# The last block's tail of a Perceiver kernel: state space prepared two pieces at a time, the perceptron begun ahead of it, its later matrices made behind its first products

## The chip, the cores and the metric

The kernel runs on one core of one Trainium2 chip. TensorE (PE), VectorE (DVE), ScalarE (ACT), GpSimd (POOL) and SyncE (SP, which issues most of the DMAs) each work through their own queue in order, and wait for each other by semaphores. The metric is the time of one execution on the device in microseconds; a kernel's time is the median of several runs. All times inside an execution are microseconds from the start of its span.

## What is computed

The network has four layers on x, 16 sequences of 64 tokens with 256 features (1024 tokens in all). Each layer is a cross attention over a context, a sequence mixer and a feed-forward part, each added to x behind a layer norm. Only the last layer matters here. Cut to that:

```python
x = x + L3_xattn(_layernorm(x), ctx)          # 8 heads of 64, 1024 keys
x = x + L3_attn(_layernorm(x))                # a state space (Mamba) block
x = x + L3_ffn(_layernorm(x))                 # a perceptron with +1/-1 matrices

# L3_attn: 512 inner channels, 16 states each
u, x_gate = split(x @ in_proj_w)              # 256 -> 512 + 512
u = silu(conv3(u) + conv_b)                   # along the 64 tokens of a sequence
delta, b, c = split(u @ x_proj_w)             # 512 + 16 + 16
delta = softplus(delta @ dt_proj_w + dt_proj_b)
h_t = exp(delta_t * a) * h_{t-1} + delta_t * b_t * u_t    # a scan over tokens
y_t = sum over the 16 states of h_t * c_t
y = (y + u * D_param) * silu(x_gate) @ out_proj_w         # 512 -> 256

# L3_ffn: kernels are booleans, w = where(kernel, 1, -1)
h = s0 * (concat([x, -x]) @ w0)               # -> 1024
h = s1 * ((relu(h) * 2) @ w1)                 # 1024 -> 1024
h = s2 * ((relu(h) * 2) @ w2)                 # 1024 -> 256
```

## The kernel before

x stays on chip as `xs`, eight tiles of 128 tokens by 256 features. The state space and the perceptron work on chunks of 256 tokens (two tiles), four chunks in all. The function `L3` runs the last layer in two phases.

In the first phase `heads64` does the attention tile by tile, and calls `go` four times a step, so that the state space of chunks already attended to runs in the gaps. In the second phase, the tail, the attention is done. `dense_setup` makes the perceptron's matrices, and then the perceptron of chunk 0, 1, 2 and 3 follows. A loop calls `go` until the state space is done with the chunk that the perceptron needs, and then once at each `yield` of the perceptron, so that what is left of chunk 2 and the whole of chunk 3 run between the perceptron's products:

```python
ssm.rate = 1.5
dense = self.dense_setup()
for i in range(0, NT, 2):
    while ssm.done < i + 2:
        ssm.go()
    for _ in dense(i, 2):
        ssm.go()
```

`go` does two things. It advances the preparation of the next chunk (`prepare`) by one piece, up to the next `yield`. And it adds `rate` to a credit, and for each whole unit of credit advances the running chunk by one item (`items`). The preparation is: norm (L1919), transposes and copies to `hTs` (L1923), eight products with the input matrix, with the convolution on VectorE (L1934, L1939) and copies on ScalarE, a Silu over all of it (L1946), the product for b and c, written to memory as `bcs` (L1953), four delta products (L1961, L1962), then the softplus: Exp (L1964), Ln (L1965), an addition on VectorE (L1966), four multiplications on GpSimd (L1969), each followed by a DMA that writes delta and delta times u to memory as `dus` (L1970).

A chunk has 32 items: eight slots of four. A slot reads its rows of `dus` back, each repeated over partitions (`rep<-dus`, L1980, eight DMAs a slot, fetched one slot ahead into four `rep` tiles); b and c come back repeated as `bc_rep` (L1992). An item is two decays on ScalarE (`da`, L2010), a product (L2016), a scan (L2020) and a product (L2023) on VectorE. Its result lies in one of six tiles `x`, taken in turn. The four results of a slot are summed on TensorE by 8 small products with `stack` (`add_up`, L2044), issued behind the second item of the next slot; so the third and fourth item of that slot take the tiles that this sum's first half sets free. After every second slot VectorE combines the sum with u and the gate (`v`, L2050, and L2051). After the last, the output product (L69 `halves<-ug`/`w,ug`) is added to x (`add_to_x`, L89), and the chunk is done.

The perceptron of a chunk (`dense`) is: norm and transposes to `hT`, layer one with 8 column blocks of 2 products, layer two with 8 blocks of 8, layer three with 2 blocks of 8, all 128 x 128 by 256 columns in float32; the profile shows two rows for each product. A block of layers one and two lands in one of four PSUM tiles `ps_h` and is taken by a relu, on ScalarE for even blocks (L2105) and on VectorE for odd ones (L2103). Layer three is added to x by VectorE (L2133), and each tile goes out by a DMA (L2136).

The perceptron's matrices come as bytes. `pack_L3_ffn` loads them into a tile of the weight ring when `dense_setup` asks for them. Then VectorE makes w0 (L2089, two pieces), ScalarE w1 (L2093, eight pieces of 128 x 1024), VectorE w2 (L2094).

The order on TensorE is the order in which the program issues, as is the work by hand in `L3` (`manual_schedule`); on the other engines and on SP's queue a scheduler may move instructions past each other.

Of the kernel before, what the change touches and what calls it, by code (L numbers as in the profile page):

```python
# [13 lines left out]
U8 = mybir.dt.uint8  # L14
# [18 lines left out]
RING = 7296  # L33
# [9 lines left out]
class Net:  # L43
# [376 lines left out]
    def heads64(  # L420
# [5 lines left out]
        nc = self.nc  # L426
        wq, wkT, wvT, wo, bo, wvo, wvo2 = self.pack()
        large = large or self.misc
        self.n_pT = 3
# [1391 lines left out]
    def pack_L3_attn(self):  # L1821

        self.slot()
        shape = {n: self.a[f"L3a_{n}"].shape for n in ("in", "bc", "out")}
        return self.carve(*shape["in"]), self.carve(128, 4, 512), self.carve(*shape["bc"]), self.carve(*shape["out"])

    def pack_L3_ffn(self):
        t = self.ring.tile([128, 4 * RING], U8, tag="w", name="w")
        got, at = [], 0
        for name, c, f in (("L3f_k0", 4, 1024), ("L3f_k1", 8, 1024), ("L3f_k2", 8, D)):  # L1830
            v = t[:, at : at + c * f].rearrange("p (c f) -> p c f", f=f)
            at += c * f
            self.nc.sync.dma_start(v, self.a[name])
            got.append(v)
        return got

    def L3(self, ctx_pool):
        tc, nc = self.tc, self.nc
        with ExitStack() as stack:
# [10 lines left out]
            with (  # L1850
                tc.tile_pool(name="sb_L3x", bufs=1, side="left", reuse_waits="tile") as self.lp,
                tc.tile_pool(name="ps_L3x", bufs=1, space=PSUM, reuse_waits="tile") as self.lps,
            ):
                self.heads64(
                    lambda shape: self.lps.tile(shape, F32, tag="t", bufs=2, name="large"),
                    ssm.go, ssm.more, ssm.first,
                )
            ctx_pool.__exit__(None, None, None)
            self.lp = pool("sb_L3f", bufs=1, side="left")
            self.lps = pool("ps_L3f", bufs=1, space=PSUM)  # L1860
            ssm.rate = 1.5
            dense = self.dense_setup()
            for i in range(0, NT, 2):
                while ssm.done < i + 2:
                    ssm.go()
                for _ in dense(i, 2):
                    ssm.go()

    def state_space(self):
        nc = self.nc  # L1870
        N = 16
        w = []
        s = SimpleNamespace(ready=0, done=0, rate=1.1, credit=0.0, prepared=0, started=0)
        al = self.sb.tile([128, 4 * N], F32, name="al")
# [31 lines left out]
        def weights():  # L1906
            for n, to in zip(("in", "bc", "out"), (w[0], w[2], w[3])):
                nc.sync.dma_start(to, self.a[f"L3a_{n}"])
            yield

        def prepare(k):
            win, wdt, wbc, _ = w
            ug = ugs[k % 2]
            os = []
            for t in range(2):
# [3 lines left out]
                nc.vector.tensor_scalar(os[t], x, mv[:, 0:1], rs, ALU.subtract, ALU.mult)  # L1919
            yield  # L1920
            hT = self.sb.tile([128, 2, CHUNK], F32, tag="hTs", name="hTs")
            for t in range(2):
                nc.scalar.copy(hT[:, :, t * 128 : (t + 1) * 128], self.transposed(os[t]))  # L1923
            yield
            up = self.act.tile([128, 4, 4, S + 2], F32, tag="hT", name="up")
# [20 lines left out]
            nc.scalar.activation(ug, ug, AF.Silu)  # L1946
            yield
            yield
            ps = self.misc([32, CHUNK])
# [131 lines left out]
    def dense_setup(self):  # L2081
        nc = self.nc
        k0, k1, k2 = self.pack()

# [6 lines left out]
        nc.vector.memset(minus, -1.0)  # L2091
        for c in range(8):
            nc.scalar.activation(w1[:, c, :], k1[:, c, :], AF.Identity, bias=minus, scale=2.0)  # L2093
        nc.vector.tensor_scalar(w2, k2, 2.0, -1.0, ALU.mult, ALU.add)  # L2094

# [11 lines left out]
        def dense(first, tiles):  # L2107
            hT = self.lp.tile([128, 2, CHUNK], F32, tag="hT", bufs=1, name="hT")
            for t in range(tiles):
# [4 lines left out]
                self.evict(hT[:, :, t * 128 : (t + 1) * 128], self.transposed(o))  # L2114
            yield

            def layer(name, w, x, chunks, k):
                r = self.lp.tile([128, 8, CHUNK], F32, tag=name, bufs=1, name=name)
                for m in range(8):
# [3 lines left out]
                    if m % 2 or chunks > 2:  # L2123
                        yield
                return r
# [3 lines left out]
            for t in range(tiles):  # L2129
# [6 lines left out]
                nc.sync.dma_start(out[:, i, :], self.xs[:, i, :])  # L2136
                yield

# [61 lines left out]
    def run(self, layers):  # L2200
# [8 lines left out]
            "L2_ffn": (self.L2_ffn, [self.pack_L2_gate] + [lambda e=e: self.pack_L2_expert(e) for e in range(E)]),  # L2209
            "L3": (None, [lambda: self.pack_heads64("L3"), self.pack_L3_attn, self.pack_L3_ffn]),  # L2210
        }
# [188 lines left out]
```

## Time and profile before

| | |
|---|---|
| median of three runs | 2966.4 us (2960.71 to 2970.5) |
| the profiled execution, whole | 2962.24 us |
| its span, first to last instruction | 2960.5 us |
| TensorE busy over the span | 2687.8 us, 91% |
| VectorE, ScalarE, GpSimd busy | 1462.2, 1045.9, 302.6 us |
| mean granted TensorE clock | 0.949 |
| last attention product ends at | 2698.24 us |
| last perceptron product ends at | 2957.20 us |

A line of a timeline gives start, length, engine, source line, operation, the written tile and the read ones, and how often; in square brackets stands how long the engine was idle before it and who released it. The windows give the busy time of each engine in a stretch of the span and the clock that TensorE was granted there, as a share of full speed. The chain that ended last is the work that, followed back from the last instruction, ended each wait.

### The profile page before, as it was taken

The page shows a single profiled execution, that of the slowest core. Times are in us where ns is not written, and L with a number is a line of the kernel's source. Part 1 is how long each engine was busy: PE and PEld are TensorE (multiplying, and loading weights), DVE is VectorE, ACT ScalarE, POOL GpSimd, SP SyncE. Part 2 cuts the span into 40 slices and gives each one's busy share as a digit, 9 for nine tenths or more (in the row PEclk, how much of TensorE's full clock was granted, in tenths as well). Part 3 has the DMA queues.
Part 4 walks back from the last instruction along what each step waited for, and adds up shares of the span by engine and source line. Part 5 has one row for each costly group of instructions (what it writes and reads, how often), then busy time and mean ns, then how long its engine had stood idle before and what let it go on. Part 6 is the DMA issues. An engine that isn't in the chain of part 4 may idle for free. (4 is left out here: it accounts for less than half of the span.)

```text
span 2960.5 us, 42845 instructions
## 1 busy us (share of the span) xinstructions
PE 2687.8 (91%) x16972; PEld 1979.6 (67%) x16972; DVE 1462.2 (49%) x3117; ACT 1045.9 (35%) x2353; POOL 302.6 (10%) x407
## 2 busy tenths in 40 slices
PE   7887997999999898989999997899998898897899
PEld 3566784666666687857776776886766566665678
DVE  3655114666666643234444344324436656658581
ACT  2322122555555431223332331122335455455330
POOL 1111223000000112310101011201001000000000
PEclk9987998999999997989999997899999999998999
DMA  9603772110100115802111112551123122121210
GB/s 237 180 34 119 267 248 70 31 37 26 37 26 23 40 36 186 277 22 66 45 45 56 54 43 93 217 195 45 47 61 92 51 79 67 48 68 54 60 34 8
DMA packets 79222, 253.57 MB, mean 86 GB/s; under 512 B 15151, under 2 KB 26955, under 8 KB 69291
## 3 DMA queue, kind: packets, MB, share of 16 engines
q1 hardware_dynamic: 59562, 165.01, 18.0%
q0 software_dynamic: 13312, 80.28, 8.0%
q10 hardware_dynamic: 6144, 5.51, 0.5%
q8 instruction: 135, 2.21, 0.3%
q14 instruction: 69, 0.56, 0.1%
HBM read 233.80 MB, written 14.82 MB: 84 GB/s over the span
## 5 line engine op out<-in xcount | busy, mean ns | idle before, releaser
L223 DVE TENSOR_REDUCE nmx<-sc 128x1 f32<-128x1024 f32 x264 | 311.7, 1218 | 226.7 <-PE sc L507 135.2
L225 ACT ACTIVATE p<-sc,nmx 128x1024 f32<-128x1024 f32 x264 | 294.6, 1116 | 315.2 <-DVE nmx L223 314.5
L507 PE MATMUL sc<-ctxT,qp 128*128 128x512 f32 (+1 forms) x1024 | 357.7, 604 | 0.0
L507 PEld LDWEIGHTS sc<-ctxT,qp 128*128 128x128 f32 (+1 forms) x1024 | 139.5, 190 | 155.2 <-issue 153.0
L69 PE MATMUL halves<-ctx,pT 128*128 128x192 f32 x1024 | 191.0, 343 | 9.4 <-DVE xs L89 4.0
L69 PEld LDWEIGHTS halves<-ctx,pT 128*128 128x128 f32 x1024 | 178.3, 203 | 12.3 <-DVE xs L89 4.5
L69 PE MATMUL misc<-ctx,pT 128*128 128x192 f32 x1024 | 177.6, 327 | 0.5 <-DVE qT L472 0.5
L235 PE MATMUL ps_t<-ident,p 128*128 128x128 f32 x1088 | 146.8, 277 | 25.3 <-ACT p L225 17.6
L69 PEld LDWEIGHTS misc<-ctx,pT 128*128 128x128 f32 x1024 | 166.3, 191 | 2.2 <-DVE qT L472 1.0
L2010 ACT ACTIVATE da<-rep,al 128x252 f32<-128x252 f32 x256 | 114.7, 498 | 114.8 <-DVE x L2020 95.3
L237 ACT COPY pT<-ps_t 128x512 f32<-128x512 f32 x182 | 104.3, 585 | 139.3 <-PE ps_t L235 137.2
L235 PEld LDWEIGHTS ps_t<-ident,p 128*128 128x128 f32 x1088 | 126.7, 142 | 39.2 <-ACT p L225 22.5
L2020 DVE TENSOR_TENSOR_SCAN x<-da,x 128x512 f32<-128x512 f32 x128 | 151.9, 1211 | 1.9 <-ACT da L2010 1.4
L235 PE MATMUL misc<-ident,p 128*128 128x128 f32 x1024 | 138.3, 280 | 13.4 <-ACT p L225 6.3
L235 PEld LDWEIGHTS misc<-ident,p 128*128 128x128 f32 x1024 | 110.7, 141 | 39.8 <-ACT p L225 14.4
L160 POOL TENSOR_TENSOR ln_rs<-ln_ve,nhalf 128x1 f32<-128x1 f32 x80 | 45.1, 569 | 725.8 <-DVE ln_ve L158 676.0
L237 ACT COPY pT<-misc 128x512 f32<-128x512 f32 x128 | 75.0, 586 | 115.5 <-PE misc L235 115.1
L69 PE MATMUL ps_h<-r,w 128*128 128x256 f32 x512 | 115.3, 385 | 0.0
L69 PEld LDWEIGHTS ps_h<-r,w 128*128 128x128 f32 x512 | 97.8, 192 | 16.6 <-issue 2.9
L69 PE MATMUL gu<-dT,wa 128*128 128x128 f32 (+1 forms) x864 | 104.9, 280 | 3.7 <-ACT dT L64 2.4
L239 DVE COPY pT<-misc 128x512 f32<-128x512 f32 x128 | 88.2, 689 | 38.9 <-PE misc L235 28.2
L69 PEld LDWEIGHTS gu<-dT,wa 128*128 128x128 f32 (+1 forms) x864 | 98.4, 185 | 10.9 <-ACT dT L64 4.8
(477 smaller groups left out, 4482.5 us busy)
## 6 DMA issues: line engine op xcount, KB each, us to landing
ctx<-in_ctx SPq DMA_DIRECT2D x48, 768.0 KB, 4.3
ctxT<-in_ctxT SPq DMA_DIRECT2D x48, 512.0 KB, 3.8
w<-in_L2f_W SPq DMA_DIRECT2D x24, 1024.0 KB, 8.6
rep<-dus SPq DMA_DIRECT2D x256, 64.0 KB, 1.9
ctxT<-in_ctxT SPq DMA_DIRECT2D x16, 768.0 KB, 14.1
ctxT<-in_ctxT SPq DMA_DIRECT2D x96, 128.0 KB, 3.6
ys<-yb ACTq DMA_DIRECT2D x40, 128.0 KB, 5.4
bc_rep<-bcs SPq DMA_DIRECT2D x32, 128.0 KB, 3.2
```

What stands on the lines that cost most here:

```text
L69: self.nc.tensor.matmul(out, lhsT, rhs, start=n == 0, stop=n == len(pairs) - 1)
L160: nc.gpsimd.tensor_tensor(rs, ve, self.nhalf, ALU.pow)
L223: self.nc.vector.tensor_reduce(nmx, sc, AX.X, ALU.max, negate=True)
L225: self.nc.scalar.activation(p, sc, AF.Exp, bias=nmx, accum_out=sums)
L235: self.nc.tensor.transpose(ps[:, u, :], p[:, at : at + 128], self.ident)
L237: self.nc.scalar.copy(pT[:, 4 * g : 4 * g + 4, :], ps)
L239: self.nc.vector.tensor_copy(pT[:, 0:4, :], ps)
L507: nc.tensor.matmul(sc[u][:, bass.ts(kh, 512)], qp[n][par][rows, h : h + 2, :].rearrange("p h q -> p (h q)"), ctx[0][rows, at], start=n == ...
L2010: nc.scalar.activation(da[:, g, :, 1:], now[j][:, 0, :].rearrange("p (b s) -> p b s", s=S)[:, :, 1:], AF.Exp, scale=al[:, col : col + 1],)
L2020: nc.vector.tensor_tensor_scan(flat, da.rearrange("p g b s -> p (g b s)"), flat, 0.0, ALU.mult, ALU.add)
```

## The change

Four things are changed, all of them in the last layer.

1. The bytes of the perceptron's matrices are fetched early. A second step of the state space's `weights` loads them with three DMAs on SP's queue at the second call of `go`, into room that is free by then: two spent weights of the attention (`wo` and `wvT`) and a new piece of the ring's tile.
2. `dense_setup` makes only w0. The eight pieces of w1 and then w2 are made by a generator, `matrices`, which is advanced at the yields of layers one and two: the even pieces of w1 on ScalarE, the odd ones and w2 on VectorE.
3. In the tail `go` is called with `hurry=2`: it advances the preparation by up to two pieces, and stops at a piece that ends with `WAIT` (the norm, the transposes, the Silu and an empty one behind it).
4. The first two yields of the first perceptron chunk run no state space. The rate is 1.4 instead of 1.5, and each yield of the perceptron gives a share of it: 0.3 behind the norm, 0.5 in layer one, 1.0 in layers two and three.

During the attention `go` is called as before, with one piece and a full share.

```diff
     def pack_L3_attn(self):
-        return self.carve(*shape["in"]), self.carve(128, 4, 512), self.carve(*shape["bc"]), self.carve(*shape["out"])
-
-    def pack_L3_ffn(self):
-        t = self.ring.tile([128, 4 * RING], U8, tag="w", name="w")
...
+        got = self.carve(*shape["in"]), self.carve(128, 4, 512), self.carve(*shape["bc"]), self.carve(*shape["out"])
+        return *got, self.carve(128, 8, 256)
+
+    def fetch_L3_ffn(self, room):
+        got = []
+        for (name, f), to in zip((("L3f_k0", 1024), ("L3f_k1", 1024), ("L3f_k2", D)), room):
+            c = self.a[name].shape[1]
+            v = to.rearrange("p c f -> p (c f)").bitcast(U8)[:, : c * f].rearrange("p (c f) -> p c f", f=f)
             self.nc.sync.dma_start(v, self.a[name])
             got.append(v)
         return got
...
-            ssm.rate = 1.5
+            ssm.rate = 1.4
             dense = self.dense_setup()
             for i in range(0, NT, 2):
                 while ssm.done < i + 2:
-                    ssm.go()
-                for _ in dense(i, 2):
-                    ssm.go()
+                    ssm.go(hurry=2)
+                for n, share in enumerate(dense(i, 2)):
+                    if i or n > 1:
+                        ssm.go(share, hurry=2)
...
             for n, to in zip(("in", "bc", "out"), (w[0], w[2], w[3])):
                 nc.sync.dma_start(to, self.a[f"L3a_{n}"])
             yield
+            self.ffn = self.fetch_L3_ffn((self.spent[0], w[4], self.spent[1]))
+            yield
...
-        def go(place=None):
-            if s.prep is None and s.prepared < NC and s.ready >= 2 * s.prepared + 2 and s.prepared <= s.done // 2 + 1:
-                s.prep = prepare(s.prepared)
-            if s.prep is not None and next(s.prep, s) is s:
-                s.prepared += s.prep.gi_code is prepare.__code__
-                s.prep = None
+        def go(share=1.0, hurry=1):
+            for _ in range(hurry):
+                if s.prep is None and s.prepared < NC and s.ready >= 2 * s.prepared + 2 and s.prepared <= s.done // 2 + 1:
+                    s.prep = prepare(s.prepared)
+                got = None if s.prep is None else next(s.prep, s)
+                if got is s:
+                    s.prepared += s.prep.gi_code is prepare.__code__
+                    s.prep = None
+                if got is WAIT:
+                    break
...
-            s.credit = min(s.credit + s.rate, 2 * s.rate)
+            s.credit = min(s.credit + share * s.rate, 2 * s.rate)
...
     def dense_setup(self):
-        k0, k1, k2 = self.pack()
+        k0, k1, k2 = self.ffn
...
-        for c in range(8):
-            nc.scalar.activation(w1[:, c, :], k1[:, c, :], AF.Identity, bias=minus, scale=2.0)
-        nc.vector.tensor_scalar(w2, k2, 2.0, -1.0, ALU.mult, ALU.add)
+        def matrices():
+            for c in range(8):
+                if c % 2:
+                    nc.vector.tensor_scalar(w1[:, c, :], k1[:, c, :], 2.0, -1.0, ALU.mult, ALU.add)
+                    yield
+                else:
+                    nc.scalar.activation(w1[:, c, :], k1[:, c, :], AF.Identity, bias=minus, scale=2.0)
+            nc.vector.tensor_scalar(w2, k2, 2.0, -1.0, ALU.mult, ALU.add)
+            yield
+
+        others = matrices()
...
-            yield
+            yield 0.3
...
                     if m % 2 or chunks > 2:
-                        yield
+                        next(others, None)
+                        yield min(1.0, chunks / 4)
...
-                yield
+                yield 1.0
```

More of the change, by code (lines that the diff above doesn't have):

```diff
@@ L427, in heads64 @@
         wq, wkT, wvT, wo, bo, wvo, wvo2 = self.pack()
+        self.spent = wo, wvT
         large = large or self.misc
@@ L1824, in pack_L3_attn @@
         shape = {n: self.a[f"L3a_{n}"].shape for n in ("in", "bc", "out")}
-        return self.carve(*shape["in"]), self.carve(128, 4, 512), self.carve(*shape["bc"]), self.carve(*shape["out"])
-    def pack_L3_ffn(self):
-        t = self.ring.tile([128, 4 * RING], U8, tag="w", name="w")
[L1829 to L1832, printed above, removed]
+        got = self.carve(*shape["in"]), self.carve(128, 4, 512), self.carve(*shape["bc"]), self.carve(*shape["out"])
[5 more added lines that the diff above has]
+            v = to.rearrange("p c f -> p (c f)").bitcast(U8)[:, : c * f].rearrange("p (c f) -> p c f", f=f)
             self.nc.sync.dma_start(v, self.a[name])
@@ L1855, in L3 @@
                     lambda shape: self.lps.tile(shape, F32, tag="t", bufs=2, name="large"),
-                    ssm.go, ssm.more, ssm.first,
+                    lambda place: ssm.go(), ssm.more, ssm.first,
                 )
@@ L1872, in state_space @@
         w = []
+        WAIT = "more would have to wait"
         s = SimpleNamespace(ready=0, done=0, rate=1.1, credit=0.0, prepared=0, started=0)
@@ L1909, in weights @@
             yield
+            self.ffn = self.fetch_L3_ffn((self.spent[0], w[4], self.spent[1]))
+            yield
         def prepare(k):
-            win, wdt, wbc, _ = w
+            win, wdt, wbc, *_ = w
             ug = ugs[k % 2]
@@ L1919, in prepare @@
                 nc.vector.tensor_scalar(os[t], x, mv[:, 0:1], rs, ALU.subtract, ALU.mult)
-            yield
+            yield WAIT
             hT = self.sb.tile([128, 2, CHUNK], F32, tag="hTs", name="hTs")
@@ L1923, in prepare @@
                 nc.scalar.copy(hT[:, :, t * 128 : (t + 1) * 128], self.transposed(os[t]))
-            yield
+            yield WAIT
             up = self.act.tile([128, 4, 4, S + 2], F32, tag="hT", name="up")
@@ L1946, in prepare @@
             nc.scalar.activation(ug, ug, AF.Silu)
-            yield
-            yield
+            yield WAIT
+            yield WAIT
             ps = self.misc([32, CHUNK])
@@ L2114, in dense @@
                 self.evict(hT[:, :, t * 128 : (t + 1) * 128], self.transposed(o))
-            yield
+            yield 0.3
             def layer(name, w, x, chunks, k):
@@ L2123, in layer @@
                     if m % 2 or chunks > 2:
-                        yield
+                        next(others, None)
+                        yield min(1.0, chunks / 4)
                 return r
@@ L2136, in dense @@
                 nc.sync.dma_start(out[:, i, :], self.xs[:, i, :])
-                yield
+                yield 1.0
         return dense
@@ L2209, in run @@
             "L2_ffn": (self.L2_ffn, [self.pack_L2_gate] + [lambda e=e: self.pack_L2_expert(e) for e in range(E)]),
-            "L3": (None, [lambda: self.pack_heads64("L3"), self.pack_L3_attn, self.pack_L3_ffn]),
+            "L3": (None, [lambda: self.pack_heads64("L3"), self.pack_L3_attn]),
         }
```

## The prediction

> **What bounds the kernel now.** I read four views in this order: the granted clock with the time of the one profiled execution, the window table of the tail cut where its character changes, TensorE's timeline there, and the chain that ended last. The instruction order of the two built kernels agrees on TensorE, VectorE, ScalarE and GpSimd up to the last addition of the last attention; only three loads on the SP queue stand earlier. So everything up to TensorE's last attention product, which ends at 2692.89 + 5.35 = 2698.24, should keep its time, and only the 259 us behind it can change.
>
> The windows (length, then busy time and count of PE, PEld, DVE, ACT, POOL, then granted clock, DMA share, GB/s):
>
> ```profile
> 2698.24:2728.91 30.67, 19.82 (x80) 14.28 (x80) 24.41 (x50) 17.57 (x31) 2.03 (x3) 0.78 0.23 80
> 2728.91:2784.25 55.34, 54.88 (x274) 44.18 (x274) 25.88 (x44) 16.63 (x26) 1.93 (x4) 1.00 0.08 20
> 2784.25:2814.80 30.55, 15.58 (x70) 8.94 (x68) 24.90 (x35) 13.73 (x31) 2.00 (x3) 0.78 0.38 112
> 2814.80:2886.30 71.50, 67.88 (x342) 52.29 (x342) 62.83 (x92) 22.35 (x51) 0.23 (x1) 0.98 0.13 34
> 2886.30:2957.20 70.90, 70.02 (x325) 60.88 (x323) 9.01 (x21) 5.59 (x12) 0.87 (x2) 1.00 0.02 6
> ```
>
> TensorE bounds three of the five stretches. In the first and third it stands still, and what it does there runs at a clock of 0.78. Its timeline shows the two holes:
>
> ```profile
> 2692.89 5.35 PE L69 MATMUL halves<-w,onT 128*128 128x256 f32 x24
> 2701.17 0.76 PE L179 MATMUL halves<-ident,o 128*128 128x128 f32 x4 [2.94 <-DVE o L2113]
> 2706.07 3.63 PE L69 MATMUL ps_h<-hT,w 128*128 128x256 f32 x8 [4.14 <-DVE w L2089]
> 2713.92 3.63 PE L2044 MATMUL halves<-x,stack 128*32 128x256 f32 x16 [3.78 <-ACT hTs L1923]
> ...
> 2785.89 1.99 PE L69 MATMUL ps_h<-hT,w 128*128 128x256 f32 x8 [0.46 <-ACT hT L64]
> 2795.96 1.06 PE L2044 MATMUL halves<-x,stack 128*32 128x256 f32 x2 [8.08 <-DVE x L2023]
> 2800.59 3.62 PE L2044 MATMUL halves<-x,stack 128*32 128x256 f32 x14 [3.58 <-DVE x L2023]
> ```
>
> The first hole is the making of the perceptron's matrices (all eight w1 pieces on ScalarE, 8 x 1.13, in front of the first relu). The second is the last chunk's preparation: its long chain starts only when TensorE has done the last delta product. The chain that ended last (start, us, what):
>
> ```profile
> 2698.67 5.79 DMA w<-in_L3f_k
> 2704.57 6.49 ACT w L2093 x7
> ...
> 2778.57 1.06 ACT du L1964
> 2779.64 1.28 ACT L1965
> 2780.94 1.16 ACT du L1965
> 2782.12 1.24 DVE du L1966
> 2783.43 2.83 POOL du L1969 x4
> 2790.52 2.04 DMA rep<-dus
> ```
>
> **A ledger of the tail.** The costliest groups behind 2698 (count; busy, mean ns):
>
> ```profile
> L69 PE MATMUL ps_h<-r,w 128*128 128x256 f32 x512 | 115.3, 385 | 0.0
> L69 PE MATMUL ps_h<-hT,w 128*128 128x256 f32 x128 | 32.7, 411 | 5.1 <-DVE w L2089 4.1 <-ACT hT L64 1.0
> L2044 PE MATMUL halves<-x,stack 128*32 128x256 f32 x192 | 29.4, 425 | 20.0 <-DVE x L2023 15.7 <-ACT hTs L1923 3.8 <-ACT ug L1943 0.5
> ```
>
> By such counts TensorE has behind 2698.24 872 rows of 256 columns (512 + 128 + 128 of the perceptron, 40 + 32 + 32 of the state space) at 3.45/16 = 0.216, 192 rows of the state sums (L2044) at 1.85/16 = 0.116, and 20 transposes at 0.19: 188.2 + 22.2 + 3.8 = 214.2 us. It ends at 2957.20, so 259.0 - 214.2 = 44.8 us are lost (a row's mean overlaps the next, so I use the rate of long runs). Counting the work done at each edge in the order of before: 15.3 are lost by 2728.9, 1.3 more by 2784.25, 19.1 by 2814.8, 7.8 by 2886.3, 1.0 to the end (44.5, the rest is rounding). The change adds no product, so I predict its losses one by one.
>
> **Part 1, the loads.** The three loads (1.8 MB) leave the tail and stand in the last block's first microseconds, behind the state space's weights. SP issues nothing between 1987.7 and 2031.5 there, so the 5.79 us that they took in the tail lie in a gap, behind some 14 us of weight products on TensorE. I take nothing; bounds 0 to 5.8, should they collide with the gathers there.
>
> **Part 2, the start.** VectorE finishes the last attention addition at 2700.78 as before (it is busy with scans until then). Its new order is w0 (2.35 for both), the constant, two normalizations (0.41 each, 0.33 apart): 2703.9. ScalarE's order has two w1 pieces (2.2) ahead of the two hT copies (0.70): from 2703.1, when the constant is there, to 2706.0. So the first product starts no earlier than before (2706.07). What goes is behind it: six column blocks instead of two before the next transposes, no 3.78 us wait and no eight-piece run in front of the relus. Half-speed products (8 rows in 3.63 against 1.73) for some 4 us bring block five to 2710.5. Block six needs VectorE's first relu, behind four w1 pieces, w2 (1.22), a norm, one scan (1.21). VectorE's w1 piece is not in the trace; bounds are 0.61 (half of w2's 1.22, the same operation) and 1.22 (w0's row, two inputs); I take 0.61, the same kind. The scan waits for ScalarE's decay behind two more w1 pieces, till 2709.9; relu ends at 2711.4. Then block six 2712.3, transposes 2713.1, blocks seven and eight 2714.8, eight products of the state space's input 2718.3. That is 11.9 us of work in 20.1: 8.2 lost against 15.3. Bounds: 7.0 (full clock at once) and 15.3 (nothing won).
>
> [...] Here GpSimd's power for the norms took 0.93 at 2703.42 beside a VectorE operation with two inputs and 0.55 alone. [...]
>
> **Part 3, the chunk's preparation ahead.** Two pieces of preparation a turn put the delta products' end after 48.4 us of tail work instead of 62.5: with 8.2 lost at 2755 instead of 2777.3. The chain (ScalarE 3.5, VectorE 1.2, GpSimd 2.8, transfers) puts the products into memory at about 2766. There a new wait comes: in SP's order two output rows of the first perceptron chunk, which wait for VectorE's final additions (2768 and 2773.3, by TensorE's order), stand ahead of two of the chunk's bc_rep loads and seven of its rep loads. So rep lands at 2773.3 + 6 issues of 0.42 + 2 = 2778, not 2768. With the table load (1.28), two decays and a relu in VectorE's queue the first scan is at 2783, not 2792.98. Four items took 8.2 there (2792.98 to 2801.15); I allow 11 with relus between: 2794. TensorE reaches the first state sum after 87.5 us of work: 2698.24 + 87.5 + 8.2 + 0.9 = 2794.8. Loss 0, with a margin of 1 us; upper bound 19.1 as before.
>
> VectorE's wait for buffers changes place too: chunk 2's remaining 11 items now wait for a sum that stands 18.9 us of work into the tail (2726), not at 2713.9. Queued behind are 11 x 2.4 us, the delta additions and relus; walked through against TensorE's order, their last pair is done at 2765 and TensorE wants it at 2767. Zero, barely covered.
>
> **Part 4, pace.** The rate of 1.4 and the shares spread the 32 items over two perceptron chunks: the seven gaps between the eight sums hold 79.4 us of TensorE work, 11.3 each. VectorE took (2878.1 - 2793.0)/8 = 10.6 a slot, relus included. So TensorE stays the bound; I allow 2 (0 to 7.8).
>
> **Part 5, joints.** A chunk's start costs 0.9 twice (2784.25 to 2785.89, less 0.76 of transposes). The last chunk now starts right behind the state space's output: before, that output ended at 2886.33 and the norm, hidden then, at 2889.41; with 1.0 from there to the first product (2914.48 to 2915.48) and 0.76 of work inside, 3.3 are lost. A hole of 2.28 us in attention (16 products in 4.55 instead of 2.77) cost 1.8 of clock, one of 2.05 at 2859.69 nothing; I take 0.9, so 4.2.
>
> [...] The rows show a drop at 2.28, so I keep it.
>
> **Sum.** 8.2 + 2 + 1.8 + 4.2 + 1 (small waits) = 17.2 lost, not 44.8: 27.6 us less. The profiled execution took 2962.24 (span 2960.5 and 1.7 around it), 4.2 under the median of the three runs, 2966.4. So 2934.6 for one like it, and against the median 2938.8; I say 2939.
>
> **Rivals.**
> 1. *The items start as late as before* (2794, SP's queue or chunk 2 late). For: the two output rows in SP's queue, margins of 1 to 2 us. Against: TensorE would have to be 11 us late. The first sums would be ready at 2802.2 with TensorE there at 2794.8: 7.4 and 1.8 of clock, then a pace that VectorE holds. 2939 + 9 = 2948.
> 2. *The start gains nothing* (ScalarE's conversions hold relus and copies as before): 15.3 instead of 8.2, 2946. For: the first product still starts at 2706. Against: only four pieces remain on ScalarE, two of them ahead of the first relu's need.
> 3. *Slower: the ring of six x buffers serializes.* Items three and four of a slot wait for the slot before's sum, which stands in TensorE's queue behind up to 10.4 us of perceptron. If VectorE could run nothing beside those, a slot cost 10.4 + 1.9 + 9.4 = 21.7, over eight slots 83 us more than 11.3: 3022. It turns slower from 11.3 + 27.6/8 = 14.8 us a slot. Against: with the same ring the stretch 2814.8 to 2886.3 has TensorE at 67.88 of 71.50.
>
> **How the numbers follow.** Forecast 0.72, rivals one and two together 0.2, an early-load collision or the like that takes most of the gain 0.04, slower 0.04. The low end is the sum of the favourable bounds (7.0 + 1.8 + 3.3 lost: 32.7 less, 2934) less 3 for the runs' spread; the high end takes both rivals, 2939 + 9 + 7 = 2955, less what both at once is unlikely to reach: 2953. A change within 0.3% (8.9 us, about what a measurement here can tell from none) needs two thirds of the gain gone.
>
> **What would show it.** Right: the windows' first stretch near 20 us for 11.9 of work, TensorE's clock 1.0 from about 2712 on, no wait of more than 2 us at the state sums, the first scan of the last chunk near 2783, and one hole of 3 to 4 us some 46 us before the end. Wrong: a hole of 5 us or more at the first state sum behind the second chunk's products, or VectorE relus late by microseconds while TensorE waits for ps_h.

## The result, and the profile after

The changed kernel takes 2944.8 us in the median of four runs (2941.7 to 2946.4), beside 2965.1 for the kernel before (the three runs known to the prediction and one more): a ratio of 0.9935 (95% interval 0.9923 to 0.9946), so 19 to 20 us faster. The forecast was 2939 with a range of 2931 to 2953. The profiled execution took 2943.5 us, its span is 2941.7.

The last attention product ends at 2694.66 + 5.35 = 2700.01, and 238.4 us follow to the end of the last perceptron product, where before had 259.0. TensorE's work there is 214.2 in both, so 24.2 are lost instead of 44.8. All of the gain, 20.6, is in the tail; 1.8 of it is given back ahead of it, where the instructions of the compute engines are the same (more on that below). The windows of the tail of the changed kernel (length, then busy time and count of PE, PEld, DVE, ACT, POOL, then granted clock, DMA share, GB/s), cut behind the input products of chunk 3, at the starts of the second and third perceptron chunks, and behind the state space's last output product:

```profile
2700.01:2720.30 20.29, 13.63 (x57) 11.46 (x58) 17.16 (x38) 10.37 (x19) 2.56 (x3) 0.83 0.02 4
2720.30:2784.12 63.82, 59.87 (x302) 46.53 (x300) 38.28 (x62) 20.70 (x36) 6.00 (x5) 1.00 0.17 52
2784.12:2834.96 50.84, 48.70 (x244) 38.98 (x244) 45.18 (x65) 22.05 (x49) 0.55 (x1) 1.00 0.21 56
2834.96:2890.85 55.89, 55.31 (x288) 43.24 (x288) 43.46 (x66) 15.05 (x34) 0.10 (x1) 1.00 0.10 29
2890.85:2938.44 47.59, 44.43 (x197) 37.98 (x196) 6.27 (x15) 4.54 (x10) 1.00 (x2) 0.96 0.01 3
```

The second stretch where TensorE stood still is gone: the granted clock is 1.00 from 2720 to 2890. The start keeps a clock of 0.83, and the last stretch now has one of 0.96. TensorE's timeline shows the holes that are left:

```profile
2705.29 1.11 PE L179 MATMUL halves<-ident,o 128*128 128x128 f32 x4 [5.28 <-DVE o L2138]
2707.78 7.05 PE L69 MATMUL ps_h<-hT,w 128*128 128x256 f32 x24 [1.38 <-ACT hT L64]
...
2745.22 1.92 PE L2054 MATMUL halves<-x,stack 128*32 128x256 f32 x16 [1.14 <-ACT du L1972]
...
2772.40 0.70 PE L69 MATMUL halves<-w,r 128*128 128x256 f32 x2 [1.00 <-DVE r L2128]
...
2775.53 3.72 PE L69 MATMUL halves<-w,r 128*128 128x256 f32 x16 [0.58 <-DVE v L2060]
...
2801.64 1.92 PE L2054 MATMUL halves<-x,stack 128*32 128x256 f32 x16
...
2834.06 0.44 PE L179 MATMUL halves<-ident,o 128*128 128x128 f32 x2 [1.68 <-DVE xs L2159]
...
2891.81 0.44 PE L179 MATMUL halves<-ident,o 128*128 128x128 f32 x2 [0.80 <-DVE o L2138]
2894.14 0.44 PE L179 MATMUL halves<-ident,o 128*128 128x128 f32 x2 [1.90 <-DVE o L2138]
2895.04 8.86 PE L69 MATMUL ps_h<-hT,w 128*128 128x256 f32 x32 [0.46 <-ACT hT L64]
```

The last chunk's first state sum (2801.64) has no bracket: it waited for nothing, where before waited 8.08 and 3.58. The group of the state sums says the same; its idle time fell from 20.0 us to 2.2:

```profile
L2054 PE MATMUL halves<-x,stack 128*32 128x256 f32 x192 | 23.0, 382 | 2.2 <-ACT du L1972 1.1 <-DVE xs L2159 0.6 <-ACT ug L1953 0.5
```

Two smaller things are new. The last perceptron chunk waits 0.80 + 1.90 + 0.46 for its own norms and then runs 32 rows in 8.86 us where the same 32 rows of the second chunk take 7.17. And in the chain that ended last (start, us, what) TensorE meets VectorE at 2772:

```profile
2762.86 1.16 ACT du L1975
2764.01 0.02 issue
2764.04 1.23 DVE du L1976
2765.26 1.73 DVE x L2026 x2
2767.00 3.27 DVE x L2030 x2
2770.27 1.68 DVE x L2033 x2
2771.95 0.41 DVE r L2128
2772.35 0.04 issue
2772.40 0.70 PE halves L69 x2
```

Two scans take 3.27 there; elsewhere a pair takes 2.33. At 2765.34 GpSimd starts its four products of delta and u, which take 5.45 us together; in the kernel before they took 2.83.

**Where the first 300 us come in.** Times of different kernels can't be compared to a microsecond. The profiled executions run the same products on TensorE up to the last attention product, and yet they differ by up to 8 us there, most of it in the first 300 us. The same TensorE instructions, against the execution of before (us later):

| instruction that starts in before at | 101 | 305 | 1900 | last attention product |
|---|---|---|---|---|
| changed kernel | 4.1 | 5.5 | 2.1 | 1.8 |
| parts 1 and 2 alone | -1.0 | -1.5 | -1.5 | -1.6 |
| parts 3 and 4 alone | -0.1 | 0.0 | 0.0 | -0.1 |
| four products on VectorE | 4.1 | 6.7 | 6.9 | 6.6 |
| copies first | 5.6 | 7.1 | 6.9 | 6.6 |
| late rate | 4.5 | 5.9 | 5.6 | 2.1 |
| all four edits | 5.2 | 6.2 | 6.4 | 6.1 |

So I compare the experiments by what TensorE loses behind its last attention product: the time from its end to the end of the last product, less 214.2. It is 44.8 before and 24.2 in the changed kernel, and it can be followed product by product: at each row, the time since the last attention product less the work done so far.

The medians alone tell little apart. Parts 1 and 2 alone and the two kernels with full shares are slower than the changed kernel, the last version is faster; every other ratio below has an interval that overlaps the changed kernel's (0.9923 to 0.9946). What a single edit is worth is therefore read from one profiled tail each.

### The profile page after: what moved, and what is told of

It is laid out like the page before. It is cut to its first block, busy times and chain, and to the rows that moved or that the text cites. A ratio compares the mean times of both kernels' runs of the same rounds, so it can differ in the third digit from the quotient of the medians.

```text
span 2941.7 us, 42834 instructions
## 1 busy us (share of the span) xinstructions
PE 2681.1 (91%) x16972; PEld 1973.5 (67%) x16972; DVE 1466.4 (50%) x3120; ACT 1043.0 (35%) x2350; POOL 306.1 (10%) x407
## 5 line engine op out<-in xcount | busy, mean ns | idle before, releaser
L235 PE MATMUL ps_t<-ident,p 128*128 128x128 f32 x1088 | 147.6, 278 | 25.2 <-ACT p L225 17.6
L235 PEld LDWEIGHTS ps_t<-ident,p 128*128 128x128 f32 x1088 | 127.4, 143 | 39.2 <-ACT p L225 22.4
```

The source lines that it names most:

```text
L235: self.nc.tensor.transpose(ps[:, u, :], p[:, at : at + 128], self.ident)
```

## Experiments

**Which part brings what.** The theory at this point was: a hole at the last chunk's first sum is what a chain of some 23 us, from the last delta product to that sum, lacks in TensorE work between the two. TensorE's order is the program's, so that work can be counted: 9.4 us before (62.5 to 71.9 us of tail work), 39.1 in the changed kernel (48.4 to 87.5).

*Parts 1 and 2 alone*: the changed kernel with the old calls of `go`. The two yields without a call, at the first two of the first perceptron chunk, stay; they belong to part 4. (Here and below, `...` in a diff stands for lines left out.)

```diff
-            ssm.rate = 1.4
+            ssm.rate = 1.5
...
-                    ssm.go(hurry=2)
+                    ssm.go()
...
-                        ssm.go(share, hurry=2)
+                        ssm.go()
```

> Parts 1 and 2 alone (early loads, matrices behind the first products, the perceptron ahead), with the old go: one piece a turn, rate 1.5, no shares. In TensorE's order the chunk's last delta product ends after 69.4 us of tail work and the first state sum stands at 75.4: 6.0 us of work between them, where before had 62.5 and 71.9, 9.4 us. Theory (a hole is what the chain from the last delta product to the first sum, 23 us, lacks in work between): the start loses 8.4 instead of 15.3, the second hole grows by 3.4 to 22.5: 3.5 us less than before, about 2961.6. Rival (the parts add up, the start's gain comes through whole): 7 less, about 2958.

Measured: 2953.8 us (before beside it 2962.0), ratio 0.9975 (0.9966 to 0.9985); 39.2 lost in the tail, 5.6 less than before, between the two. The mechanism is neither. The start does lose less, 9.1 by the first state sum. But the first sums of the last chunk are ready at 2799.44 - 2696.66 = 102.8 us behind the attention, in before at 2800.59 - 2698.24 = 102.4: TensorE arrives there as late as in before (89.7 us behind the attention in both) and waits as long (8.41 + 3.58 us instead of 8.08 + 3.58), but by then it has done 3.5 us more work, since so much more stands ahead of the first sum. Between the first and the second sum stand 8.7 instead of 5.2, where before waited for another 2.49; behind the second sum it is 8.2 ahead of before. At the third chunk's sums it then waits 2.10 + 1.27, so that 5.6 are left at the end.

*Parts 3 and 4 alone*: the kernel before with the new `go` and the shares, as in the changed kernel, but with a call at every yield.

```diff
-            ssm.rate = 1.5
+            ssm.rate = 1.4
...
-                    ssm.go()
-                for _ in dense(i, 2):
-                    ssm.go()
+                    ssm.go(hurry=2)
+                for n, share in enumerate(dense(i, 2)):
+                    ssm.go(share, hurry=2)
```

> Parts 3 and 4 alone on the kernel before (two pieces a turn, shares, rate 1.4; late load, matrices all ahead, no skipped yields). 42.5 us of work stand between the last delta product (41.5) and the first sum (84.0). Theory: no hole there, the start stays at 15.3, and what the changed kernel loses later stays (about 13.3 with the joints at 2.9 and 5.2): 28.6 lost instead of 44.8, about 2949. Rival (the two parts need each other, since the two pieces a turn queue behind ScalarE's eight matrix pieces): the start loses up to 5 more, 2954.

Measured: 2943.0 us, ratio 0.9942 (0.9922 to 0.9962); 24.7 lost. That is 20.1 of the 20.6 without early loads, and with all eight pieces of w1 on ScalarE in one run. TensorE's timeline at the start:

```profile
2705.95 3.67 PE L69 MATMUL ps_h<-hT,w 128*128 128x256 f32 x8 [4.13 <-DVE w L2096]
2709.45 0.60 PE L179 MATMUL halves<-ident,os 128*128 128x128 f32 x4
2709.89 1.89 PE L69 MATMUL ps_h<-hT,w 128*128 128x256 f32 x8
2713.82 3.72 PE L69 MATMUL halves<-hTs,w 128*128 128x256 f32 x16 [2.03 <-ACT hTs L1925]
```

The copy of `hTs` comes at 2713.8 as before. But the shares of 0.3 and 0.5 keep the state sum out of this place; two more blocks of layer one fill 1.9 us of the wait at full speed, and from 2713.8 on TensorE runs at full speed too, where before needed until about 2720. 10.7 are lost here, not 15.3: the shares alone bring 4.6 of the 6.9 us gained at the start, all of which the prediction put down to part 2. Parts 1 and 2, with the two skipped yields, bring 6.1 (9.2 lost there), so the gains overlap.

*One piece at a time*: the changed kernel with `hurry=1` in both calls.

```diff
-                    ssm.go(hurry=2)
+                    ssm.go(hurry=1)
...
-                        ssm.go(share, hurry=2)
+                        ssm.go(share, hurry=1)
```

> The changed kernel with one piece of preparation a turn. The last delta product ends at 66.0 us of work instead of 48.4, the first sum stays at 87.5: 21.5 us between. Theory (it is the pace that closes the second hole; the chain needs 23): hole of 0 to 4, at most 1.8 of clock, about 2947 (2945 to 2950). Rival (the two pieces a turn close it, as the prediction has it): the chain starts 17.6 us later and takes the 34 us that it takes in the changed kernel to its first scan: hole of 17 and more, 2962.

Measured: 2945.6 us, ratio 0.9941 (0.992 to 0.9962); 27.2 lost, 3.0 more than the changed kernel. The last chunk's first sum waits for nothing with 21.5 us of work ahead of it, as the theory had it, and the rival is out. Up to the second chunk's start it loses only 0.3 more: 2.56 of waiting for VectorE's addition to x there (0.30 in the changed kernel), but not the 1.00 and 0.58 ahead of it. Then come 0.88 of waiting for a relu and 1.7 of half speed behind the third chunk's start (below). The medians, 2945.6 and 2944.8, do not tell the two kernels apart, and behind the same hole of 1.68 the changed kernel kept full speed (last section), so these 3.0 us are those of one execution.

```profile
2802.32 1.92 PE L2054 MATMUL halves<-x,stack 128*32 128x256 f32 x16
...
2835.76 0.44 PE L179 MATMUL halves<-ident,o 128*128 128x128 f32 x2 [1.68 <-DVE xs L2159]
2836.66 5.41 PE L69 MATMUL ps_h<-hT,w 128*128 128x256 f32 x16 [0.46 <-ACT hT L64]
```

*Full shares*: the changed kernel with rate 1.5 and no shares, `hurry=2` kept.

```diff
-            ssm.rate = 1.4
+            ssm.rate = 1.5
...
-                        ssm.go(share, hurry=2)
+                        ssm.go(hurry=2)
```

> The changed kernel with rate 1.5 and full shares, two pieces a turn kept. The last delta product ends at 50.3, the first sum stands at 73.6: 23.3 us of work between; last output product at 144.5 instead of 172.2, so the last perceptron chunk's joint is covered. Theory (the two output rows in SP's queue hold the chunk's loads back until about 2780, whenever the delta products are made): hole of 10 to 13 and 1.8 of clock at the first sum, pace of VectorE costs 7.8, last joint 4.2 less: about 2960. Rival (the loads are not held back; the chain takes its 23 us from the delta products): no hole, 7.8 - 4.2 more: 2948.

Measured: 2956.1 us, ratio 0.9979 (0.9967 to 0.9991); 38.7 lost. From the second chunk's start to behind the second sums 12.2 go, so the hole is back although the preparation runs two pieces at a time:

```profile
2793.26 0.62 PE L2054 MATMUL halves<-x,stack 128*32 128x256 f32 x2 [1.45 <-DVE x L2033]
2797.90 3.35 PE L2054 MATMUL halves<-x,stack 128*32 128x256 f32 x14 [4.02 <-DVE x L2033]
```

Of the two halves of the idea, the pace is the one that closes the hole. But is it the output rows in SP's queue that held the chain back here, as the theory said?

**Are the chunk's loads held back?** *The run just shown, with output rows on GpSimd's queue*; and *the changed kernel with that edit alone*:

```diff
-                nc.sync.dma_start(out[:, i, :], self.xs[:, i, :])
+                nc.gpsimd.dma_start(out[:, i, :], self.xs[:, i, :])
```

> The kernel of the run with rate 1.5 and full shares (hole of 12.2 us at the last chunk's first sums), with the output rows issued on GpSimd's queue instead of SP's; all else as there. Theory (two output rows in SP's queue held the last six rep loads of the first slot back until VectorE had finished both rows): all eight loads are issued without a stop, about 5.5 us earlier, and the first sums with them: hole of 6 to 7, about 2950. Rival (ScalarE's table load, decays and VectorE's queue set it, not the loads): hole 10 or more, 2955.

> The changed kernel with the output rows issued on GpSimd's queue instead of SP's, nothing else. Theory (the rows held the last chunk's loads back, but at this pace TensorE does not reach the first sum before it is ready): first scan of the last chunk about 85 us behind the last attention product instead of 91.5, and the same time as the changed kernel within 1.5, 2943 to 2946. Rival (the held loads cost time in the changed kernel as well, through VectorE): 3 us less, 2942.

Measured: 2961.4 us for the first, ratio 0.9985 (0.9971 to 1.0), 39.1 lost; its hole is 11.0 instead of 12.2, but 1.7 more are lost right ahead of it, at the second chunk's start, where TensorE waits 2.12 instead of 0.46 for ScalarE's copy to `hT`, which the first decays now precede. Nothing is gained, so that theory falls. 2948.0 us for the second, ratio 0.9946 (0.9929 to 0.9963), 24.1 lost, as much as without the edit; but the first scan moved by 1.8 only, not by 6.5. The loads did go out without a stop, yet the work behind them did not follow. ScalarE and VectorE in the second:

```profile
2786.39 0.37 ACT L64 COPY hT<-halves 128x256 f32<-128x256 f32 x1 [18.59 <-PE halves L179]
...
2790.93 1.28 ACT L2020 ACT_TABLE_LOAD   x1
...
2791.70 1.28 DVE L2026 TENSOR_TENSOR x<-rep,bc_rep 128x512 f32<-128x512 f32 x2
2793.16 1.23 DVE L2030 TENSOR_TENSOR_SCAN x<-da,x 128x512 f32<-128x512 f32 x1 [0.17 <-ACT da L2020]
```

ScalarE idles for 18.59 us, takes the perceptron's copies and two relus, and only then loads the table for the first decays, which stand behind them in its queue. In before, one piece, the changed kernel, full shares, and full shares without output rows on SP, the first scan comes 94.7, 93.5, 91.5, 85.8 and 85.0 us behind the attention: close together, while the last delta product moves from 66.0 us of work (one piece) to 48.4 (two pieces). Only with parts 3 and 4 alone, where the delta products end at 41.5, did the first items get in ahead of the second chunk's norms and copies: 76.9. So the first sum's place in TensorE's order decides, far more than the chain's start: 71.9 us of work in before and 73.6 with full shares come too early, 87.5 does not.

**What the changed kernel still loses.** *The four products of delta and u on VectorE*, for the last chunk:

```diff
-                nc.gpsimd.tensor_tensor(e[:, c, :], dl[:, c, :], ug[:, c, :], ALU.mult)
+                (nc.vector if k == NC - 1 else nc.gpsimd).tensor_tensor(e[:, c, :], dl[:, c, :], ug[:, c, :], ALU.mult)
```

> The changed kernel with the last chunk's four products of delta and u on VectorE instead of GpSimd. Theory (in the changed kernel these four met VectorE's scans and products and both went slow: 5.45 us instead of 2.83 on GpSimd, 3.35 instead of 2.33 for two scans, and TensorE then waited 1.00 and 0.58 for VectorE at 2772 and 2775): the scans take 2.33 a pair again, the two waits go, 1 to 2 us less than the changed kernel: about 2943. Rival (the slow scans have another cause, such as the transfers; the four products just lengthen VectorE's queue by 4 x 0.42 = 1.7): the scans stay at 3.35, 1 to 2 us more than the changed kernel: about 2946.5.

Measured: 2941.2 us, ratio 0.9911 (0.988 to 0.9943); 23.6 lost, 0.6 less. The changed kernel first, then this one (GpSimd and VectorE, then VectorE):

```profile
2765.34 5.45 POOL L1979 TENSOR_TENSOR du<-du,ug 128x256 f32<-128x256 f32 x4 [49.42 <-DVE du L1976]
2766.92 3.35 DVE L2030 TENSOR_TENSOR_SCAN x<-da,x 128x512 f32<-128x512 f32 x2
```

```profile
2770.59 1.42 DVE L1979 TENSOR_TENSOR du<-du,ug 128x256 f32<-128x256 f32 x4
2771.93 1.22 DVE L2030 TENSOR_TENSOR_SCAN x<-da,x 128x512 f32<-128x512 f32 x1
```

A scan takes 1.22 again, so the theory's cause is shown. Its size was less than hoped: the wait of 1.00 at layer three fell to 0.43, the one of 0.58 stayed. Beside each other both were slow: 5.45 against 2.83 in before for GpSimd's four products, 3.35 against 2.33 elsewhere for two scans. The prediction had GpSimd's power at the start, 0.93 beside a VectorE operation against 0.55 alone, and missed the like here.

*Copies first*: w0 (made in `first_matrix`) behind the two norms of the first perceptron chunk, and the constant of ScalarE's pieces made from `hT`, so that they can't be ahead of its copies.

```diff
...
+            if not first:
+                first_matrix()
+                nc.scalar.activation(minus, hT[:, 1, 255:256], AF.Copy, scale=0.0, bias=-1.0)
             yield 0.3
```

> The changed kernel with w0 made behind the first chunk's two norms, and ScalarE's constant made from hT, so that the copies to hT stand ahead of ScalarE's w1 pieces. Theory (the early bytes let VectorE make w0, 2.35 us, ahead of the norms, and ScalarE two pieces of w1 ahead of the copies, so the first product came no earlier): transposes 3 us behind the attention instead of 5.3, first product 5.6 behind it instead of 7.8, and the start loses 6.2 to 6.9 instead of 8.4: about 2943. Rival (VectorE's first relu, behind four w1 pieces, w2 and a scan, sets the start): first product 2 us earlier, but the loss at the second transposes stays 8 to 8.7: 2944.8.

Measured: 2941.1 us, ratio 0.9916 (0.9892 to 0.994); 21.0 lost, 3.2 less than the changed kernel.

```profile
2707.80 0.76 PE L179 MATMUL halves<-ident,o 128*128 128x128 f32 x4 [2.93 <-DVE o L2139]
2709.35 7.09 PE L69 MATMUL ps_h<-hT,w 128*128 128x256 f32 x24 [0.79 <-DVE w L2107]
2716.28 0.60 PE L179 MATMUL halves<-ident,os 128*128 128x128 f32 x4
```

The attention ends at 2704.87 here: the first product starts 4.5 behind it instead of 7.8, the second transposes 11.4 instead of 14.7. All 3.3 us reach the end. So what held the start of the changed kernel was not VectorE's first relu, as the prediction had it, but w0 ahead of the norms and two w1 pieces ahead of the copies.

*A faster pace, to put work behind the output product*: rate 1.55 throughout with output rows on GpSimd's queue, and rate 1.65 from the ninth yield of the second perceptron chunk on, alone.

```diff
-            ssm.rate = 1.4
+            ssm.rate = 1.55
```

```diff
+                    if i == 2 and n == 9:
+                        ssm.rate = 1.65
                     if i or n > 1:
```

> The changed kernel at rate 1.55 (shares kept), with the output rows on GpSimd's queue. In TensorE's order the first sum of the last chunk stands at 80.6 us of work instead of 87.5, the last at 158.4 instead of 168.7, and the output product ends at 165.3, with 6.9 us of products of layer three behind it, where it ended at 172.2 right ahead of the last perceptron chunk. Theory (the last joint's 5.2 are lost because nothing stands behind the output product; VectorE holds 10.6 a slot against 10.8 of TensorE; the loads without a stop bring the first scan to about 2784): no wait at the first sums, last joint 1, 4 us less than the changed kernel: about 2941. Rival (VectorE can't hold the pace beside the relus): waits of 1 to 3 us at each sum, up to 8 lost, 2947 to 2950.

> The changed kernel with the rate raised from 1.4 to 1.65 from the ninth yield of the second perceptron chunk on. The first two sums of the last chunk stay where they were (87.5 and 99.7 us of work), the last moves from 166.9 to 160.0, the output product from 168.7 to 161.8, ahead of the whole of layer three (6.9), and one sum comes to stand between layer three and the third chunk's start. Theory (the two joints lost 5.2 and 2.9 for want of work behind them): last joint 1, the other 1, waits of at most 3 at the sums: 18 to 21 lost instead of 24.2, about 2940. Rival (VectorE then holds TensorE up at the sums for as much as the joints give): 24, 2945.

Measured: 2943.7 us, ratio 0.9925 (0.99 to 0.9949), 24.4 lost, for the first; 2940.1 us, ratio 0.9921 (0.9905 to 0.9938), 23.8 lost, for the second. Both cover the last joint: it loses about 1 instead of 5. Both lose it again. At 1.55 the first sum comes too early once more (7.0 lost from the second chunk's start to the second sum). At 1.65 a sum stands between layer three and the third chunk's transposes and waits for the half bank that VectorE has yet to add to x:

```profile
2837.11 3.10 PE L2056 MATMUL halves<-x,stack 128*32 128x256 f32 x16 [4.74 <-DVE xs L2161]
```

VectorE is at more items by then: between its two additions to x (2832.00 and 2836.58) stand two scans and three products.

*All four edits*: copies first, four products on VectorE, output rows on GpSimd's queue, rate 1.65 as above.

> The changed kernel with all of these: w0 behind the norms and the copies ahead of ScalarE's w1 pieces, the last chunk's four products of delta and u on VectorE, output rows on GpSimd's queue, rate 1.65 from the ninth yield of the second perceptron chunk on. Theory (the gains lie in different stretches and add: 3.3 at the start, 0.7 at the four products, 4.2 and 2 at the joints, no wait at the sums because the first scan comes 6 us and more earlier): 13 to 15 lost instead of 24.2, about 2935. Rival (VectorE's pace takes the place): waits of 4 to 6 at the sums, about 2940.

Measured: 2946.0 us, ratio 0.9939 (0.9922 to 0.9955); 20.5 lost. The gains at the start (3.3) and at the four products (0.6) add; the joint's are eaten by the same wait of 4.74 as above. The time is 11 above the expectation. The tail explains about 6 of them (20.5 lost, not 13 to 15); in the profiled execution the part up to the attention's end was 6.1 longer than before's. The tail itself is 3.8 shorter than the changed kernel's.

*The last version*: copies first, four products on VectorE, and the rate raised only where the order up to the third chunk's start stays as it was.

```diff
+                    if i == 4 and n == 5:
+                        ssm.rate = 2.0
                     if i or n > 1:
```

> The changed kernel with w0 behind the norms and the copies ahead of ScalarE's w1 pieces, the last chunk's four products of delta and u on VectorE, and the rate raised to 2.0 from the fifth yield of the third perceptron chunk on, so that everything up to that chunk's start keeps its order and only the last three sums move (158.1 to 151.2, 166.9 to 160.0 us of work) and the output product (168.7 to 161.8), ahead of layer three. Theory (start, the four products and the last joint add: 3.3, 0.7 and 4.2, and VectorE, at 10.6 a slot from the first scan on, comes at most 2 late for the last sums): 16 to 18 lost behind the attention instead of 24.2. With the first 300 us as in the median of the runs that is 6 to 8 less than the changed kernel, about 2938. Rival (VectorE is as late at the last sums as the joint gives): 20 lost, 2941.

Measured: 2932.0 us (2928.8 to 2936.5; before beside it 2960.6), ratio 0.9896 (0.988 to 0.9913); 15.4 lost. It is ahead of both kernels. Its last joint:

```profile
2877.59 3.72 PE L69 MATMUL halves<-w,ug 128*128 128x256 f32 x16
2881.15 7.07 PE L69 MATMUL halves<-w,r 128*128 128x256 f32 x32
2888.05 0.38 PE L179 MATMUL halves<-ident,o 128*128 128x128 f32 x2
2888.79 0.44 PE L179 MATMUL halves<-ident,o 128*128 128x128 f32 x2 [0.36 <-DVE xs L2165]
2889.69 7.17 PE L69 MATMUL ps_h<-hT,w 128*128 128x256 f32 x32 [0.46 <-ACT hT L64]
2896.70 27.79 PE L69 MATMUL ps_h<-r,w 128*128 128x256 f32 x128
```

Layer three (7.07) covers the norms that the changed kernel waited for; what is left is 0.36 + 0.46, and the 32 rows take 7.17, not 8.86. No sum waits, though the last four follow each other at 8.95 us (2848.87, 2857.83, 2866.78, 2875.74), less than the 10.6 that VectorE takes a slot: its items were ahead by then.

## Why the prediction was right, and where it was not

**The size.** 20.6 us gained in the tail against 27.6; the kernel landed inside the range, above its middle. TensorE is the bound, its work is the same, and two holes were the thing to count: that held. Of the signs that the prediction named, the start of 20.3 us, the clock of 1.00 from 2711 on, sums without a wait above 2 us, and the hole some 46 us before the end came; a first scan near 2783 did not.

**Part 1, the loads at nothing:** held. The TensorE instruction that starts at 1900 in before is 2.1 later in the changed kernel, and so is the one at 2101 (2.0); the three loads are issued between, at 1990.

**Part 2, the start, 8.2 lost by the end of the input products:** 8.4 measured. But the working was right by accident, and the gain is not part 2's alone. The working let block six wait for VectorE's first relu, done at 2711.4, 13.2 behind the attention. In the run that relu ran from 11.5 to 11.9 behind it, and nothing waited for it: all six blocks (24 rows) ran on end in 7.05 us, the first 3.3 of them at half speed (clock 0.50 up to 2711.08). By the prediction's own rates, 8 rows in 3.63 us for 4 us and then in 1.73, five blocks are done at about 2712.5, not at 2710.5; this slip and the wait that did not exist made up for each other. What did hold the start, w0 and two w1 pieces ahead of the first product, the working had at its beginning; moving them took away 3.3. And parts 3 and 4 alone bring the start to 10.7, while parts 1 and 2 alone, with the two yields skipped, bring it to 9.2: the two halves overlap. Parts 1 and 2 added 2.3 there and 0.5 in the end: between there and the second chunk's start the changed kernel loses 1.6 more than parts 3 and 4 alone do (5.5 against 3.9). GpSimd's power for the norms took 1.46 us at 2708.50 beside VectorE's w2, and 0.55 at 2714.23 alone; that cost nothing.

**Part 3, the preparation ahead, first scan at 2783, 84.8 behind the attention:** the step that failed. It came 91.5 behind. What failed are the 5 us between the landing of the loads (2778) and the first scan (2783), counted as a table load, two decays and a relu:

```profile
2788.28 1.28 DVE L2026 TENSOR_TENSOR x<-rep,bc_rep 128x512 f32<-128x512 f32 x2
...
2789.23 1.28 ACT L2020 ACT_TABLE_LOAD   x1
...
2791.46 1.22 DVE L2030 TENSOR_TENSOR_SCAN x<-da,x 128x512 f32<-128x512 f32 x1 [1.90 <-ACT da L2020]
```

VectorE's first product on the loaded rows ran at 2788.28 without a wait, but the scan behind it waited 1.90 for ScalarE's decay. ScalarE took the second perceptron chunk's two copies and three of its relus first (the last at 2788.74), then loaded its table. These copies and relus waited for products of TensorE, which was itself some 5 us late. The prediction walked through SP's queue, but not through ScalarE's. So a chain that starts 17.6 us of work earlier ended 2.0 earlier (91.5 against 93.5 with one piece at a time), and the two output rows in SP's queue were worth 1.8; they too came later than predicted, 73.6 and 79.8 behind the attention instead of about 70 and 75. Loss 0 at the first sum was right all the same, because part 4 moved that sum to 87.5 us of work and TensorE was some 5 us late by then. That is not luck alone, since the scan that follows TensorE's copies and relus comes earlier when TensorE does: in the last version TensorE reaches the sum at 97.7 behind the attention, the first scan comes at 87.6, and no sum waits. With one piece at a time the loss there is also 0.

**Part 4, pace, 2 lost:** no sum waited for its items. Priced as the spreading of 32 items, it was in truth the cause of the second hole's end and, alone, worth some 4.6 at the start.

**Part 5, joints.** 0.9 + 0.9 + 4.2. Measured: 0.8 at the second chunk; 2.1 at the third, where VectorE's addition to x stands behind two scans; 3.2 of waiting at the fourth and 1.7 of clock. The mechanism at the fourth held, 0.7 too small.

**The small terms.** The allowance of 1 for small waits met 0.46, 1.14, 1.00, 0.58 and 0.58: 3.8. And 44.8 is a remainder, which holds everything that the work counts leave out, while 17.2 was a list: about 4 us in the changed kernel lie in no wait and in no slow stretch but in gaps of a few hundredths up to 0.4 between 53 groups of rows. The list compared with the remainder had to come out too good. With 3.5 for these gaps behind the start, 2.8 for waits, 1.2 and 0.6 for joints, 0.2 for the start and 2 less for the pace, 6.3 of the 7.0 are found.

**The rivals.** Items as late as before (first scan 94.7): nearly so, at 91.5, but it cost nothing: the price was worked out for a TensorE on time, and TensorE came about 5 us later. The start gaining nothing: out. The ring that serializes: out; sums 12.2 us of work apart saw no wait, and in the last version 8.95.

## What to carry over

Count, in the order of the engine that bounds, how much of its work stands between a chain's start and the first instruction that needs its end; where an instruction is asked for matters more here than how early its inputs are begun, since each engine in between takes its own queue in order (ScalarE's table load for the first decays, at 2789.23, stood behind two copies and three relus). Test the parts of a change alone before crediting one: here 20.1 of 20.6 came with half of the edits. And compare a list of losses with a list, a remainder with a remainder.

## What the runs showed of the hardware beyond expectation

**Half speed without a long hole.** TensorE went to half speed behind 0.80 + 1.90 + 0.46 us of waiting (last joint), and with one piece at a time behind a longest single hole of 1.68:

```profile
2836.60:2839.00 2.40, 2.34 (x8) 2.02 (x9) 2.40 (x4) 1.92 (x6) 0.00 (x0) 0.75 0.40 109
2839.00:2842.50 3.50, 3.50 (x15) 2.42 (x16) 1.01 (x3) 0.73 (x2) 0.00 (x0) 0.68 0.00 0
```

(Same columns as the windows above; the hole ends at 2835.76.) Yet the same hole of 1.68 in the changed kernel, and one of 2.05 in before (ahead of 2859.69), were followed by full speed. So the length of one hole does not decide here. In the traces of before and of the changed kernel every stretch of half speed within the span lasts 3.41 us or a whole multiple of it (33 and 34 stretches), and the stretches of one execution lie on one grid of that step, so the grid tells how busy TensorE was in the window ahead:

| window of 3.41 us, us | what falls into it | TensorE busy, us | clock in the next window |
|---|---|---|---|
| one piece at a time, 2834.41:2837.82 | 1.35 of its hole of 1.68, and 0.46 | 1.59 | 0.50 |
| changed kernel, 2830.54:2833.96 | 1.58 of its hole of 1.68 | 1.84 | 1.00 |
| before, 2856.00:2859.42 | 1.78 of its hole of 2.05 | 1.64 | 1.00 |
| changed kernel, last joint, 2891.98:2895.40 | 1.90 and 0.46 | 1.06 | 0.50 |

Behind the last attention product the two traces have 130 such windows at full speed: the six in which TensorE was busy for less than 1.3 us were followed by half speed, the other 124, each busy for more than 1.6, by full speed. So in these executions the clock went with TensorE's busy time in the window ahead, and thus with where a hole fell; why is not shown. One window at half speed cost the last joint 1.7 us (8.86 against 7.17). The prediction took 0.9 for the clock at the fourth chunk, between 1.8 and nothing; the chunk paid 1.7.

**The first 300 us.** Executions with the same instructions there differ by up to 8.6 us in the table (-1.5 to 7.1 at 305), as much as half of this change's gain. Why was not tried; the tail's losses, in contrast, repeat closely: the start is 8.7 at the second transposes in all nine profiled kernels that share it.
